# Moving one-hots and clearing to ScalarE, and 95 instead of 83 groups as dense matrices, in a four-layer graph network

## The chip, the cores and the metric

The kernel runs on one core of one Trainium2 chip. A core has five engines that run their own instruction queues and meet through semaphores: PE (TensorE, matrix products; PEld is its loading of weights), DVE (VectorE), ACT (ScalarE), POOL (GpSimd) and SP (SyncE, which here only issues DMAs). The metric is the device time of one execution in microseconds (us). Before the change it is 8078.04 us, the median of 14 runs (8072.22 to 8087.21).

## The reference, cut to what matters

There are 12500 nodes with 128 features and 200000 edges. The edges are sorted by `dst`, and `dst` is 12500 times the square of a uniform number, so low nodes have very many edges and high nodes have few. `src` is uniform. Four layers follow each other; after each, a normalization over the features of a node.

```python
# layer 0
W = silu(dist_feat @ fw1 + fb1) @ fw2 + fb2          # one row per edge, from 50 features
x = silu(h @ aw1 + ab1) @ aw2 + ab2                  # one row per node
agg = segment_sum(W * x[src], dst)
out = silu(agg @ ow1 + ob1) @ ow2 + ob2;  return h + out
# layer 1: the edges the other way round
out = segment_sum(x[dst], src)
# layer 2
agg = segment_sum(edge_weight[:, None] * x[src], dst)
h = (agg + x) @ W1.T + b1 + agg * x @ W2.T + b2;  out = leaky_relu(h, 0.2)
# layer 3: 16 relations, each with its own 128 x 128 matrix
srcs = alphas[rels] * srcs_dense[rels, src]
vrps = segment_sum(srcs, dst) + (vfts @ update)[dst] added once per edge;  out = relu(vrps)
# each layer
x = layernorm(x + layer(x))
```

Layers 1 and 2 are products of `x` with a sparse 12500 x 12500 matrix: layer 1 with the counts of edges between two nodes, layer 2 with the sums of their weights.

## The kernel before

**Edges and groups.** 512 edges make a group of four columns of 128 edges; there are NG = 391 groups and T = 1564 columns. Because the edges are sorted, the edges of a group fall into a window of 128 consecutive nodes. Each layer walks the groups from the highest to the lowest in a loop over steps `s`. In each step several stages work, each on another group: `group(k)` is the group that has reached stage `k`. Everything is written in this order into the queues of the engines (`tc.manual_schedule()`), and each engine runs its queue in order. The order of the calls in the loop body is thus the order on each engine.

**Layer 0 (steps 0 to 402).** Stage 0 loads the edge features `dt`; stage 2 computes `ph` on PE (one PSUM buffer); stage 3 applies silu on ACT (`h`, L766) and gathers 4 x 128 rows of the node table on POOL (`gather`, L305, into a buffer of the pool `xg`); stage 5 computes `pw` on PE (L770, L773); stage 7 builds one-hots of the target nodes on DVE (`one_hots`, L322) and multiplies `pw` with the gathered rows (L780); stage 8 sums them by target node on PE (L346); stage 11 adds the window to `acc` (L371). Besides, `blk.run(s)` finishes the nodes in blocks of 128, from the highest, as their last group is done: product and silu (L699), root on ACT with a reload of ACT's function tables before and after it (L639, L766), norm (L647), and stores on SP.

**Layer 1 (from step 392).** `L1 = NG + 1`. For each group, ACT builds two one-hots (L1013, L1015, L1017), PE multiplies them to counts, ACT copies the counts (L790), PE multiplies them with a window of the table, ACT copies the result into a buffer of the pool `xg` (L833), and POOL adds its rows by DMA into one of four sums in memory (`scatter_add`, L393). DVE computes the addresses (`twins_by_group`, `to`, L1026, nine buffers).

**Dense matrices for the lowest nodes.** The groups below GH = 83 hold so many edges per node that their part of the sparse matrix is built as dense blocks instead. `dense_plan()` cuts the first HC = 332 columns of edges into HBATCHES = 24 batches; each batch covers at most HS = 32 target nodes, and a batch has units of 4, 2, 1 or 0 columns (0 stands for a column that is cut into two halves of 64 edges), such that the edges of a unit lie within HW = 5 nodes. `DenseSteps` does it twice in one tile `dense` of 128 x 98 x 32 numbers: kind 0 (the counts of layer 1, in bf16 one-hots) runs in the steps of layer 0, kind 1 (the weights of layer 2, in f32) in the steps of layer 1. Per unit there are three calls:

- `make`, given in step `s`: for each column a one-hot `dense_lo` (128 wide, L930) and a one-hot `dense_hi` (490 wide, L933 for kind 1, L936 for kind 0), both on DVE, four buffers each;
- `multiply`, given in step `s + 1`: their product on PE (`du`, L951);
- `add`, taken in step `s + 2`: DVE adds `du` to five of the 32 columns of `dense` (L962).

Behind a batch whose last unit is made in step `s`, `store` (step `s + 3`) writes `dense` to memory on SP's queue (L967, 1568 KB) and `clear` (step `s + apart + 2`) sets it to zero on DVE (L971). The next batch is begun in step `s + 1 + apart`. `rate` is the number of steps from one unit (or one pair of units of four columns at most) to the next.

```python
for kind, t, apart, rate in ((0, 8.0, 4, 1.68), (1, first_weights, 3, 1.2)):
```

`todo.take(s)` runs the calls taken in a step in the middle of the loop body, behind stage 11 of layer 0; `todo.give(s, ...)` runs those given at the end, `make` last.

From step 417 on the counts are used: for each of the 98 blocks of source nodes and each of ROUNDS = 2 rounds of HB = 12 batches, SP loads a part of the counts (`dense_in`, for two blocks at a time), ACT brings it into line (`dense_line`, L986), PE transposes it (L994), ACT copies it (`dense_t`, L998), PE multiplies it with the rows of the low nodes (L1004), and DVE adds the product to `x` (L1007). One block of one round goes in each step. The weights are used in layer 2 in the same way, without a transpose (`dense_w_in`, L1212), one block of one round in each step, and their sums are added to `acc` behind that.

**Between and behind.** `nodes_1` adds up the four sums and normalizes. Layer 2 walks the groups down to GH: gathers on POOL, weighted one-hots on DVE (L328), sums on PE (L346), add to `acc` (L371); blocks of nodes are finished as their groups are done (`finish_steps`), and the table of relations for layer 3 is written. Layer 3 gathers from that table for all 391 groups. `gather` and the messages of layer 1 share the pool `xg`: seven buffers, each with the 512 rows of a group.

Of the kernel before, what the change touches and what calls it, by code (L numbers as in the profile page):

```python
# [8 lines left out]
F32 = mybir.dt.float32  # L9
# [8 lines left out]
P = 128  # L18
# [20 lines left out]
HS = 32  # L39
HB = 12  # L40
ROUNDS = 2
# [6 lines left out]
class Consts:  # L48
    def __init__(self, nc, pool):
        self.ident = pool.tile([P, P], F32, name="ident")  # L50
        make_identity(nc, self.ident)
        self.row = pool.tile([P, P], F32, name="row")
        nc.gpsimd.iota(self.row, pattern=[[1, P]], base=0, channel_multiplier=0,
                       allow_small_or_imprecise_dtypes=True)
        self.nodes = pool.tile([P, NB + 1], F32, name="nodes")
        nc.gpsimd.iota(self.nodes, pattern=[[P, NB + 1]], base=0, channel_multiplier=1,
                       allow_small_or_imprecise_dtypes=True)
        self.ones = pool.tile([P, P], F32, name="ones")
# [4 lines left out]
        nc.vector.memset(self.eps, EPS)  # L63

        self.before = pool.tile([P, P], BF16, name="before")
        nc.vector.tensor_scalar(self.before, self.row, self.nodes[:, 0:1], None, op0=OP.is_lt)
# [89 lines left out]
class Edges:  # L156
# [24 lines left out]
    def steps(self, wk, ps):  # L181
# [25 lines left out]
        base = wk.tile([1, NG], F32, name="base_f")  # L207
        nc.vector.tensor_copy(base, self.base)
        pb = by_group("pb")
        nc.tensor.matmul(pb, c.ones[0:1, :], base, start=True, stop=True)  # L210
# [4 lines left out]
        nc.tensor.matmul(px, c.ones[0:1, :], step, start=True, stop=True)  # L215
        yield
# [227 lines left out]
def kernel(ctx: ExitStack, tc: tile.TileContext, i, out):  # L444
# [204 lines left out]
    def row_block(table, b):  # L649
        return table[b * P:(b + 1) * P, :]  # L650

    def windows():
        with tc.manual_schedule():
            with tc.tile_pool(name="pa", bufs=3) as wk, tc.tile_pool(name="pas", bufs=4) as small, \
                    tc.tile_pool(name="pd", bufs=2) as dn, tc.tile_pool(name="pps", bufs=2, space=PSUM) as ps:
                layers_0_and_1(wk, small, dn, ps)
            with tc.tile_pool(name="pn", bufs=4) as wk, tc.tile_pool(name="pns", bufs=4) as small, \
                    tc.tile_pool(name="pnps", bufs=3, space=PSUM) as ps:
                nodes_1(wk, small, ps)
            with tc.tile_pool(name="pb", bufs=2) as wk, tc.tile_pool(name="pbk", bufs=1) as kp, \  # L660
                    tc.tile_pool(name="pbs", bufs=4) as small, tc.tile_pool(name="pbps", bufs=2, space=PSUM) as ps:
                layers_2_and_3(wk, kp, small, ps)
# [5 lines left out]
    def layers_0_and_1(wk, small, dn, ps):  # L668
# [20 lines left out]
        def b_copy(b):  # L689
            t = bst[b]["a"] = small.tile([P, P], F32, name="a", tag="a", bufs=2)  # L690
            nc.vector.tensor_copy(t, acc[:, b * P:(b + 1) * P])
# [5 lines left out]
        def b_silu(b):  # L697
            h = bst[b]["h"] = small.tile([P, P], F32, name="hb", tag="hb", bufs=2)
            nc.scalar.activation(h, fixed[:, 0, :], AF.Silu, bias=w.ob1)  # L699
# [34 lines left out]
        srcs = {}  # L734
        SC = 64

# [124 lines left out]
    class DenseSteps:  # L861
# [4 lines left out]
        def __init__(self, dn, ps, dense, fixed, first_weights, first_products):  # L866
# [10 lines left out]

            for kind, t, apart, rate in ((0, 8.0, 4, 1.68), (1, first_weights, 3, 1.2)):
                for b, units in enumerate(DENSE):
                    k = 0  # L880
                    while k < len(units):
# [8 lines left out]
                        t += rate  # L890
                    self.later(self.given, s + 3, self.store, kind, b)
                    self.later(self.taken, s + apart + 2, self.clear)
                    t = s + 1 + apart
# [29 lines left out]
        def make(self, kind, unit):  # L923
# [4 lines left out]
            for col in range(c0, c0 + n):  # L928
                lo = self.tile("dense_lo", P, dtype)
                nc.vector.tensor_scalar(lo, c.row, ed.dense_lo[:, col:col + 1], None, op0=OP.is_equal)  # L930
                hi = self.tile("dense_hi", J * P, dtype)[:, :NB * HW]
                if kind:
                    nc.vector.tensor_scalar(hi, self.key, ed.dense_key[:, col:col + 1], ed.dense_w[:, col:col + 1],  # L933
                                            op0=OP.is_equal, op1=OP.mult)
                else:
                    nc.vector.tensor_scalar(hi, self.key, ed.dense_key[:, col:col + 1], None, op0=OP.is_equal)  # L936
                made.append((lo, hi))
# [31 lines left out]

        def clear(self):  # L970
            nc.vector.memset(self.dense, 0.0)  # L971

# [11 lines left out]
        def line_up(self, h):  # L984
            self.line[h] = self.dn.tile([P, HB, HS], F32, name="dense_line", tag="dense_line")
            nc.scalar.copy(self.line[h], self.chunk[h // 2][:, :, h % 2, :])  # L986
# [673 lines left out]
    with tc.If(fits > 0) as arm:  # L1660
        with tc.tile_pool(name="xg", bufs=7) as gp:
            windows()
    with arm.Else():
# [52 lines left out]
```

## Time and profile before

| | |
|---|---|
| median of 14 runs | 8078.04 us |
| the profiled execution, its own time | 8083.42 us |
| span of its profile | 8081.6 us |
| PE, DVE, ACT, POOL busy | 72%, 50%, 33%, 76% of the span |
| layer 0, first to last gather | 75 to 2097 us |
| layer 1, first to last scatter | 2112 to 4426 us |
| layer 2, first to last gather | 4528 to 6076 us |
| layer 3, first gather to the end | 6109 to 8082 us |

A group of instructions is shown as: line, engine, operation, out<-in xcount | busy us, mean ns of one | idle time of the engine just ahead of them and what ended it. "issue" is time in which the engine waited for nothing that the profile shows. In a view by time, a row gives the start in us, the length in us, and in brackets the idle time ahead of it and what released it. Matmul ends are modelled, so a busy PE is not a PE at its peak. The granted clock is a share of TensorE's full speed.

### The profile page before, as it was taken

The page shows a single profiled execution, that of the slowest core. Times are in us where ns is not written, and L with a number is a line of the kernel's source. Part 1 is how long each engine was busy: PE and PEld are TensorE (multiplying, and loading weights), DVE is VectorE, ACT ScalarE, POOL GpSimd, SP SyncE. Part 2 cuts the span into 40 slices and gives each one's busy share as a digit, 9 for nine tenths or more (in the row PEclk, how much of TensorE's full clock was granted, in tenths as well). Part 3 has the DMA queues.
Part 4 walks back from the last instruction along what each step waited for, and adds up shares of the span by engine and source line. Part 5 has one row for each costly group of instructions (what it writes and reads, how often), then busy time and mean ns, then how long its engine had stood idle before and what let it go on. Part 6 is the DMA issues. An engine that isn't in the chain of part 4 may idle for free. (4 is left out here: it accounts for less than half of the span.)

```text
span 8081.6 us, 89625 instructions
## 1 busy us (share of the span) xinstructions
PE 5820.9 (72%) x24309; PEld 3794.1 (47%) x24309; DVE 4068.4 (50%) x14132; ACT 2628.1 (33%) x5986; POOL 6122.5 (76%) x5603
## 2 busy tenths in 40 slices
PE   8888888898787766777643677777776666666665
PEld 5555555555444444554332344444443444444343
DVE  6776666654576555545431444445444443433333
ACT  2333333221577776777663311111110000000000
POOL 4777777777788888888887477777776777777777
PEclk8888888777898877777555898987775555555555
DMA  5543333333467677776655666664442222222221
GB/s 152 171 153 100 99 99 92 98 94 91 86 123 134 122 130 126 123 131 111 104 89 78 213 172 168 170 170 138 131 127 71 59 58 58 57 56 55 55 54 51
DMA packets 877253, 882.01 MB, mean 109 GB/s; under 512 B 428177, under 2 KB 683624, under 8 KB 870598
## 3 DMA queue, kind: packets, MB, share of 16 engines
q0 software_dynamic: 316960, 366.85, 24.6%
q1 hardware_dynamic: 545705, 496.90, 20.3%
q10 hardware_dynamic: 14078, 12.43, 0.5%
q8 instruction: 202, 3.31, 0.2%
q14 instruction: 308, 2.52, 0.1%
HBM read 555.71 MB, written 319.97 MB: 108 GB/s over the span
## 5 line engine op out<-in xcount | busy, mean ns | idle before, releaser
L305 POOL DMA_INDIRECT xg<-table,at x2796 | 2720.7, 973 | 952.9 <-issue 730.0
L346 PE MATMUL pa<-oh,xg 128*128 128x128 f32 x5592 | 1691.0, 418 | 1052.6 <-DMA xg<-rel_table,at 623.5
L393 POOL DMA_INDIRECT sums<-xg,to x1232 | 1913.6, 1553 | 414.8 <-issue 295.8
L346 PEld LDWEIGHTS pa<-oh,xg 128*128 128x128 f32 x5592 | 1185.8, 273 | 1638.3 <-issue 717.3
L305 POOL DMA_INDIRECT xg<-rel_table,at x1564 | 1485.3, 950 | 477.1 <-issue 374.5
L371 DVE TENSOR_TENSOR acc<-acc,pa 128x128 f32 x1090 | 305.9, 281 | 1422.4 <-PE pa L346 1365.9
L328 DVE TENSOR_SCALAR oh<-row,drel,wgt 128x128 f32<-128x128 f32 x2796 | 793.2, 359 | 34.3 <-PE pa L346 26.5
L951 PE MATMUL du<-dense_hi,dense_lo 128*128 128x490 f32 (+3 forms) x1239 | 706.2, 661 | 86.9 <-DVE dense L962 85.0
L647 ACT ACTIVATE x<-x,off,rs 128x128 f32<-128x128 f32 x294 | 144.9, 493 | 1392.1 <-DVE off L646 1384.5
L830 PE MATMUL fixed<-oh,one_b 128*1 128x128 bf16 x1216 | 144.9, 256 | 595.7 <-DVE m L1021 591.3
L783 PE MATMUL ph<-dt,fw 50*128 50x512 f32 x782 | 500.2, 723 | 75.2 <-ACT h L766 67.5
L773 PE MATMUL pw<-fw,h 128*128 128x128 f32 x3128 | 552.6, 330 | 0.0
L773 PEld LDWEIGHTS pw<-fw,h 128*128 128x128 f32 x3128 | 466.1, 229 | 115.0 <-issue 115.0
L346 PE MATMUL pa<-oh,m 128*128 128x128 f32 x3128 | 505.1, 315 | 12.8 <-DVE acc L371 12.8
L346 PEld LDWEIGHTS pa<-oh,m 128*128 128x128 f32 x3128 | 474.0, 232 | 14.6 <-DVE acc L371 14.1
L639 ACT ACTIVATE rs<-mv,eps 128x1 f32<-128x1 f32 x294 | 86.8, 295 | 1203.9 <-DVE mv L634 1185.9
L962 DVE TENSOR_TENSOR dense<-dense,du 128x490 f32 x646 | 427.8, 662 | 91.4 <-PE du L954 71.2
L1026 DVE TENSOR_TENSOR to<-n_ahead,at 128x4 int32<-128x4 f32 x308 | 50.6, 164 | 838.8 <-DMA sums<-xg,to 833.4
L780 DVE TENSOR_TENSOR m<-pw,xg 128x512 f32<-128x512 f32 x391 | 268.0, 685 | 395.0 <-DMA xg<-table,at 375.4
L1013 ACT ACTIVATE oh<-row,drel 128x128 bf16<-128x128 f32 x1216 | 388.7, 394 | 218.4 <-PE fixed L830 213.1
L1161 PE MATMUL pr<-wrel,x 128*128 128x512 f32 x784 | 435.5, 685 | 2.3 <-ACT x L1153 2.3
L766 ACT ACTIVATE h<-ph,fb 128x512 f32<-128x512 f32 x391 | 266.6, 682 | 510.2 <-PE ph L783 508.1
(205 smaller groups left out, 8436.2 us busy)
## 6 DMA issues: line engine op xcount, KB each, us to landing
rel_table<-tb SPq DMA_DIRECT2D x196, 512.0 KB
dt<-in_src_r SPq DMA_DIRECT2D x308, 256.0 KB
xg<-table,at POOLq DMA_INDIRECT x2796
dt<-in_dfT SPq DMA_DIRECT2D x391, 100.0 KB
dense_counts<-dense SPq DMA_DIRECT2D x24, 1568.0 KB
dense_in<-dense_counts SPq DMA_DIRECT2D x98, 384.0 KB
dense_weights<-dense SPq DMA_DIRECT2D x24, 1568.0 KB
dense_w_in<-dense_weights SPq DMA_DIRECT2D x96, 384.0 KB
```

The source lines that it names most:

```text
L305: nc.gpsimd.indirect_dma_start(out=x[:, j, :], out_offset=None, in_=table, in_offset=bass.IndirectOffsetOnAxis(ap=idx[:, j:j + 1], axis=0))
L328: nc.vector.tensor_scalar(oh[:, j, :], c.row, at[:, j:j + 1], weight[:, j:j + 1], op0=OP.is_equal, op1=OP.mult)
L346: self.nc.tensor.matmul(pa, x[:, j, :], oh[:, j, :], start=j == 0, stop=j == J - 1)
L371: nc.vector.tensor_add(to, to, pa)
L393: nc.gpsimd.indirect_dma_start(out=accs[(first + j) % len(accs)], out_offset=bass.IndirectOffsetOnAxis(ap=to[:, j:j + 1], axis=0), in_=msg ...
L773: nc.tensor.matmul(pw[:, j, :], h[:, j * P:(j + 1) * P], w.fw2, start=False, stop=j == J - 1)
L780: nc.vector.tensor_mul(ms[g], pws.pop(g), xgs.pop(g))
L783: nc.tensor.matmul(phs[g], w.fw1, dts.pop(g), start=True, stop=True)
L951: nc.tensor.matmul(pk[:, :NB * HW], lo[part], hi[part], start=j == 0, stop=j == len(made) - 1)
L962: nc.vector.tensor_tensor(to, to, pk[:, :NB * HW].rearrange("p (h n) -> p h n", n=HW), op=OP.add)
L1013: nc.scalar.activation(pair[:, 0, j, :], c.row, AF.Abs, bias=at[:, j:j + 1], scale=-1.0)
L1161: nc.tensor.matmul(pr, t["x3"], wrel[:, k:k + 4, :], start=True, stop=True)
```

## The change

It has five parts.

1. HB goes from 12 to 16. With that there are 32 batches, HC = 380 columns and GH = 95 groups. The 48 new columns are all of kind "0": two halves each, so 96 more products and adds for each kind. Layers 1 and 2 walk 296 groups, not 308. The tiles that hold all batches of a round are a third wider: `dense_in`, `dense_line`, `dense_t`, the product of layer 2 (512 columns, not 384).
2. The times of `DenseSteps`: `rate` 1.68 becomes 1.32 and 1.2 becomes 1.0; `apart` 4 becomes 3 and 3 becomes 2; `store` is given in step `s + 2`, not `s + 3`.
3. `make` of kind 0 builds each one-hot on ACT with two instructions, Abs of the difference and Relu of one less that, instead of one comparison on DVE.
4. `clear` is two copies of a zero on ACT, each of half of `dense`, in steps `s + 4` and `s + apart + 2`, instead of one memset on DVE.
5. Room in SBUF: the pool `xg` has six buffers in layers 0 and 1 (seven in layers 2 and 3, where it is opened anew behind `nodes_1`); `a`, `hb` and `dense_line` have one buffer, not two; the sources are loaded and converted for 16 columns at a time, not 64 (`sources`, DMA on SP, cast on ACT); `ones` is one column, and a row of ones is made where it is needed.

```diff
-HB = 12
+HB = 16
...
-            with tc.tile_pool(name="pa", bufs=3) as wk, tc.tile_pool(name="pas", bufs=4) as small, \
+            with tc.tile_pool(name="xg", bufs=6) as gp, tc.tile_pool(name="pa", bufs=3) as wk, tc.tile_pool(name="pas", bufs=4) as small, \
...
-            with tc.tile_pool(name="pb", bufs=2) as wk, tc.tile_pool(name="pbk", bufs=1) as kp, \
+            with tc.tile_pool(name="xg", bufs=7) as gp, tc.tile_pool(name="pb", bufs=2) as wk, tc.tile_pool(name="pbk", bufs=1) as kp, \
...
-            t = bst[b]["a"] = small.tile([P, P], F32, name="a", tag="a", bufs=2)
+            t = bst[b]["a"] = small.tile([P, P], F32, name="a", tag="a", bufs=1)
...
-            h = bst[b]["h"] = small.tile([P, P], F32, name="hb", tag="hb", bufs=2)
+            h = bst[b]["h"] = small.tile([P, P], F32, name="hb", tag="hb", bufs=1)
...
-        SC = 64
+        SC = 16
...
-            for kind, t, apart, rate in ((0, 8.0, 4, 1.68), (1, first_weights, 3, 1.2)):
+            for kind, t, apart, rate in ((0, 8.0, 3, 1.32), (1, first_weights, 2, 1.0)):
...
-                    self.later(self.given, s + 3, self.store, kind, b)
-                    self.later(self.taken, s + apart + 2, self.clear)
+                    self.later(self.given, s + 2, self.store, kind, b)
+                    self.later(self.taken, s + 4, self.clear, 0)
+                    self.later(self.taken, s + apart + 2, self.clear, 1)
...
-                nc.vector.tensor_scalar(lo, c.row, ed.dense_lo[:, col:col + 1], None, op0=OP.is_equal)
                 hi = self.tile("dense_hi", J * P, dtype)[:, :NB * HW]
                 if kind:
+                    nc.vector.tensor_scalar(lo, c.row, ed.dense_lo[:, col:col + 1], None, op0=OP.is_equal)
                     nc.vector.tensor_scalar(hi, self.key, ed.dense_key[:, col:col + 1], ed.dense_w[:, col:col + 1],
                                             op0=OP.is_equal, op1=OP.mult)
                 else:
-                    nc.vector.tensor_scalar(hi, self.key, ed.dense_key[:, col:col + 1], None, op0=OP.is_equal)
+
+                    for to, of, at in ((lo, c.row, ed.dense_lo), (hi, self.key, ed.dense_key)):
+                        nc.scalar.activation(to, of, AF.Abs, bias=at[:, col:col + 1], scale=-1.0)
+                        nc.scalar.activation(to, to, AF.Relu, bias=c.ones[:, 0:1], scale=-1.0)
...
-        def clear(self):
-            nc.vector.memset(self.dense, 0.0)
+        def clear(self, k):
+
+            half = self.dense.rearrange("p h n -> p (h n)")[:, k * NB * HS // 2:(k + 1) * NB * HS // 2]
+            nc.scalar.copy(half, c.zero.to_broadcast([P, NB * HS // 2]))
...
-            self.line[h] = self.dn.tile([P, HB, HS], F32, name="dense_line", tag="dense_line")
+            self.line[h] = self.dn.tile([P, HB, HS], F32, name="dense_line", tag="dense_line", bufs=1)
...
-        with tc.tile_pool(name="xg", bufs=7) as gp:
-            windows()
+        windows()
```

More of the change, by code (lines that the diff above doesn't have):

```diff
@@ L57, in __init__ @@
                        allow_small_or_imprecise_dtypes=True)
-        self.ones = pool.tile([P, P], F32, name="ones")
+        self.ones = pool.tile([P, 1], F32, name="ones")
         nc.vector.memset(self.ones, 1.0)
@@ L63, in __init__ @@
         nc.vector.memset(self.eps, EPS)
+        self.zero = pool.tile([P, 1], F32, name="zero_c")
+        nc.vector.memset(self.zero, 0.0)
         self.before = pool.tile([P, P], BF16, name="before")
@@ L208, in steps @@
         nc.vector.tensor_copy(base, self.base)
+        ones = wk.tile([1, P], F32, name="ones_row")
+        nc.vector.memset(ones, 1.0)
         pb = by_group("pb")
-        nc.tensor.matmul(pb, c.ones[0:1, :], base, start=True, stop=True)
+        nc.tensor.matmul(pb, ones, base, start=True, stop=True)
         step = wk.tile([1, NG], F32, name="step")
@@ L214, in steps @@
         px = by_group("px")
-        nc.tensor.matmul(px, c.ones[0:1, :], step, start=True, stop=True)
+        nc.tensor.matmul(px, ones, step, start=True, stop=True)
         yield
@@ L650, in row_block @@
         return table[b * P:(b + 1) * P, :]
+    gp = None
     def windows():
+        nonlocal gp
         with tc.manual_schedule():
-            with tc.tile_pool(name="pa", bufs=3) as wk, tc.tile_pool(name="pas", bufs=4) as small, \
+            with tc.tile_pool(name="xg", bufs=6) as gp, tc.tile_pool(name="pa", bufs=3) as wk, tc.tile_pool(name="pas", bufs=4) as small, \
                     tc.tile_pool(name="pd", bufs=2) as dn, tc.tile_pool(name="pps", bufs=2, space=PSUM) as ps:
```

## The prediction, made before the result was known

> **What bounds the kernel now.** I read the busy time by stage first, then the costliest groups, then single engines in order of time where two of them meet. Stages, in order: two parts of layer 0, the dense part of layer 1, layer 2 (columns: stretch, length, busy PE, PEld, DVE, ACT, POOL with instruction counts, granted clock, DMA share, GB/s).
>
> ```profile
> 98.00:400.00 302.00, 268.03 (x1311) 169.28 (x1310) 217.32 (x744) 93.15 (x134) 229.59 (x238) 0.88 0.49 153
> 800.00:2097.00 1297.00, 1125.92 (x5169) 751.16 (x5168) 757.45 (x2430) 379.90 (x564) 991.92 (x1002) 0.81 0.33 95
> 2246.00:3770.00 1524.00, 1111.55 (x5973) 735.42 (x5972) 844.56 (x2482) 1125.11 (x2869) 1254.89 (x808) 0.81 0.70 126
> 4528.00:6077.00 1549.00, 1126.07 (x4377) 736.12 (x4377) 742.72 (x2822) 220.45 (x572) 1173.62 (x1232) 0.84 0.54 152
> ```
>
> POOL looks 76 to 82% busy, but the rest is the issue of its own next DMA. In order of time its gathers of layer 0 start every 1.25 us with "issue" between them, and one thing only disturbs them (POOL, then DVE):
>
> ```profile
> 551.59 0.95 POOL L305 DMA_INDIRECT xg<-table,at  x1 [0.30 <-DVE oh L322]
> 552.84 3.99 POOL L305 DMA_INDIRECT xg<-table,at  x1 [0.30 <-issue]
> 557.13 0.94 POOL L305 DMA_INDIRECT xg<-table,at  x1 [0.30 <-issue]
> ...
> 553.26 2.67 DVE L971 MEMSET dense<- 128x3136 f32 x1 [0.60 <-issue]
> ```
>
> A gather that meets the clearing of `dense` takes 4 us, not 0.94. So POOL sets the pace: 4 x 1.25 = 5.0 us a step in layers 0 and 2 (measured in layer 2: 1.257 us from start to start), and 4 x 1.85 = 7.4 us in layer 1, whose scatters start every 1.85 us. Layer 3 is the same gathers and is not touched. Cheaper work on another engine gains nothing unless it shortens POOL; dearer work costs nothing until it falls behind POOL's pace. PE runs its steps in 3.4 to 4.3 us where nothing stops it (starts of `h` at 121.30, 124.65, 128.93, 132.28). ACT is the engine with room in layer 0, and has little in layer 1.
>
> **The change part by part**, against the profiled execution's own 8083.4 us, which is 5.4 us above the median 8078.0.
>
> *Clears leave DVE (layer 0).* 24 starts of gathers in layer 0 lie over 1.6 us apart, each at an L971; what they exceed 1.25 by sums to 56 us. On ACT the copies run beside POOL as its silus do: -56. Ends: 0 (a copy holds POOL as well) and -56. The scatters of layer 1 keep 1.54 us and a pitch of 1.85 beside a clear, so nothing there.
>
> *Counts' one-hots leave DVE.* Gathers away from the clears exceed 0.94 us by 19 us in total; the 233 beside L936 by 0.04 each. -9, ends 0 and -19.
>
> *The same one-hots on ACT.* A column is Abs and Relu of 128, Abs and Relu of 490, each Relu waiting for its Abs. The rows:
>
> ```profile
> L1013 ACT ACTIVATE oh<-row,drel 128x128 bf16<-128x128 f32 x1136 | 363.1, 395 | 165.3 <-PE fixed L830 160.1 <-DVE n_ahead L1024 5.2
> L766 ACT ACTIVATE h<-ph,fb 128x512 f32<-128x512 f32 x383 | 261.1, 682 | 475.6 <-PE ph L783 473.5
> L639 ACT ACT_TABLE_LOAD x97 | 124.5, 1283 | 1.7
> ...
> 2610.00 1.26 ACT L1015 ACTIVATE oh<-dt,src_f 128x128 bf16<-128x128 int32 x4
> 2611.29 1.15 ACT L1017 ACTIVATE oh<-oh,ones 128x1024 bf16<-128x1024 bf16 x1
> ...
> 150.90 1.12 PE L783 MATMUL ph<-dt,fw 50*128 50x512 f32 x2
> 151.95 1.00 PE L951 MATMUL du<-dense_hi,dense_lo 128*128 128x490 bf16 x4
> ```
>
> Independent activations follow each other 0.1 us before the end (4 of 128 in 1.27); a dependent one 0.03 after it (1017 after 1015). So 0.39 + 0.03, then 0.30, then 0.67 (490 wide, between 0.395 and 0.682) + 0.03, then 0.58: 2.0 us a column, 8.0 for a step of four. Four columns fill all four buffers of `dense_lo` and `dense_hi`, so the next make waits for the first product of the last one, which PE issues after `ph`, and `ph` has one buffer and waits for the silu behind the last make. The loop of such a step: silu 0.69, then `ph` and the first product, 1.5 us at the clock of this row and 2.2 at 0.6 of full speed (I take 1.9, since PE will wait more and the clock is 0.57 where PE is half busy, at 3770 to 4427 us), then 8.0. That is 10.6 us, against POOL's 5.0.
>
> In steps 8 to 63 (the first four batches) there are 34 make-steps of four columns: 360 us. Two of two columns at 4.7: 9. Four gaps of three steps without a make, at PE's pace (silu, three `ph` of 1.12, products 0.93, twice 2.2 of `pw` and `pa`): 9.4 each, 37. Six halves of a clear at about 1.55 (1568 elements, by the slope from 128 to 1024 wide): 9. The first half waits for the store, which is issued one step later than it could be by little: a store issued at 2294.1 released its clear at 2302.7, so 8.6 us, some 5 of them waited, three times: 15. Fourteen blocks with two table loads, root, norm and silu, 3.5 each, one hidden in every gap: 35. Together 465 us for 56 steps that POOL does in 280: 185 late. POOL is level with ACT at step 8 (its group 4.75 at 98.5 us) and six buffers let it run two steps ahead of DVE, which is 1.5 ahead of ACT: 3.5 steps, 17 us, are free. 168 remain. Behind that, a batch of ten steps with two-column makes is 6 x 4.7 + 1.9 + 9.4 + clears 3.1 + store 5 + two blocks 7 = 54 against 50; the nine batches to step 158 differ, and I put 3 on each: 27. From step 159 on a make is one column and ACT has room. +195. Ends: ACT's instructions back to back without any wait, at 1.73 a column, are 326 us for 56 steps: +29; with the clock at 0.5 and 8 us on each later batch: +290. I take the value by the loop because each of its waits has a named queue.
>
> A rule beside that row: the Trainium skill, "TensorE: Matmul & The Clock Gate", Part 1, has the clock at full or at half, by whether PE was busy in the last window, with no value between. The trace's stages lie between (0.81, 0.57) as means. By the rule a PE that waits most of each loop would be at half: 0.8 us more in 34 loops and 28 in the gaps, which would make the sum 55 us larger.
>
> *96 more half-column products, 96 more adds, earlier rates (layer 0).* PE 96 x 0.43 and DVE 96 x 0.66 less 319 us of L930, L936, L971: behind POOL, nothing. Without that cover, PE at 89% would bind first.
>
> *12 fewer groups in layer 1.* 48 scatters at 1.85: -89, with their DMAs on SP, copies, one-hots and twins. *32 stores of weights, not 24:* 15 long gaps of POOL just after a store sum to 24 us; eight more stores, +8 (ends 0 and +30, as the loads of counts grow by a third while DMA is 70% busy). *ACT in layer 1:* a step of the products runs 2608.40 to 2614.65 when ACT is pressed, 6.25 us. To it come 0.2 (two copies 512 wide, not 384), 0.2 (a fourth transpose ahead of it), 0.34 (two half clears in nine steps), 0.28 (55 more casts of sources, 0.23 + 1.28 waited each, over 296 steps; SP issues each one step ahead at most) and about 0.27 (a clear behind its store, 2.5 us in nine steps): 7.54 against 7.4. In the 209 steps of the products: +29, ends 0 and +60. What is queued behind these ACT waits is the copy of counts and of messages, so PE's products and POOL's scatters; four steps of lead in `to` cover single waits, not a rate.
>
> *12 fewer groups in layer 2.* 48 gathers at 1.257: -60. The dense product widens from 384 to 512, 0.15 us on PE twice a step: behind POOL. Tail between the layers: the last block starts 10 steps behind the last gather, not 8: two light steps, +3, ends 0 and +6. POOL's idle 33 us there stays otherwise, as do the 101 us at the norm.
>
> *Fewer buffers, reopened pools, smaller constants:* `xg` 6 is counted above; one buffer for `a`, `hb` and `dense_line` puts back-to-back uses three steps, or one, apart: 0 (up to +5 in layer 1).
>
> Sum: 8083.4 - 56 - 9 + 195 - 89 + 8 + 29 - 60 + 3 = 8104; less 5.4 for the median: **8099 us**.
>
> **The rivals.** *Faster: the loop is shorter than its parts.* If makes cost little more than ACT's own instructions (+60 and not +195) and layer 1 stays with POOL, the sum is 7935. For it: POOL has run at 1.25 us through every other disturbance, and ACT is 30% busy there. Against: one buffer of `ph` and four of the one-hots. It decides from +173 in steps 8 to 158 downward (layer 1 as forecast). *Slower by more: layer 1 passes to ACT.* +60 there, DMA gaps +30, the loop as forecast: 8150; with the clock at half in layer 0, 8205. For it: ACT's 74% in the third window. Against: POOL's waits for ACT are nearly nil now. *The change doesn't do what it says: the ACT copy holds POOL as the memset did.* +56 and a third more for 32 batches: 8174. Against it: no gather is long beside an ACT instruction.
>
> **How the numbers follow.** Forecast 0.42, own range 8050 to 8150; faster 0.35, centred on 7950; layer 1 on ACT 0.18; POOL held 0.05. This kernel's runs tell about 0.2%, 16 us. From these: faster 0.36 (the rival and the low edge of the forecast), within 16 us 0.15, slower 0.49. Two in ten left out at the edges of both outer cases gives 7965 to 8200.
>
> **What would show it.** Right: gathers in the first 600 us that wait, with ACT over 85% busy there and starts of `h` some 10 us apart in make-steps; no gather over 2 us beside a clear; 296 x 7.4 us of scatters; layer 2 about 58 us shorter. Wrong: POOL at 1.25 us from step 8 on; or scatters apart by more than 1.95 us on average between 2300 and 3800; or a granted clock that stays at 0.88 in the first batches, which would take 40 us off the loop.

## The result, and the profile after

| | |
|---|---|
| median after | 8166.72 us (8152.51 to 8174.23, 6 runs) |
| median before, same chip | 8077.56 us |
| ratio | 1.0108, 95% interval 1.0098 to 1.0118 |
| span of the profile after | 8173.9 us (before 8081.6) |

The change makes the kernel slower by 1.1%: 89 us, where 21 were forecast. The stages, read from the starts of POOL's instructions (us):

| stretch | before | after | difference | forecast |
|---|---|---|---|---|
| layer 0, first to last gather | 2022.4 | 2229.5 | +207 | +130 |
| layer 1, first to last scatter | 2313.5 | 2247.1 | -66 | -52 |
| layer 2, first to last gather | 1547.9 | 1484.7 | -63 | -60 |
| last gather of layer 2 to first of layer 3 | 33 | 50 | +17 | +3 |
| all else | | | -3 | 0 |

The forecast of layer 0 is -56 -9 +195, that of layer 1 -89 +8 +29. Layer 0 differs most from what was said, by 77 us. Layer 1 and the tail behind layer 2 differ by 14 each, with opposite signs.

The stages after, as they were shown of before (stretch, length, busy PE, PEld, DVE, ACT, POOL with instruction counts, granted clock, DMA share, GB/s); the first rows are layer 0:

```profile
98.00:250.00 152.00, 104.55 (x387) 61.51 (x387) 36.25 (x119) 120.79 (x236) 76.59 (x82) 0.72 0.22 65
250.00:500.00 250.00, 170.22 (x633) 101.55 (x632) 74.51 (x261) 192.42 (x352) 101.92 (x109) 0.69 0.32 102
500.00:750.00 250.00, 197.42 (x836) 126.32 (x836) 109.07 (x380) 183.44 (x317) 142.64 (x152) 0.77 0.47 151
750.00:1000.00 250.00, 204.61 (x966) 129.93 (x965) 131.26 (x445) 203.48 (x349) 171.36 (x181) 0.86 0.34 101
...
2320.00:4566.00 2246.00, 1713.71 (x8624) 1098.21 (x8623) 1189.17 (x3636) 1684.76 (x4050) 1835.70 (x1183) 0.77 0.69 124
4668.00:6153.00 1485.00, 1106.37 (x4234) 697.51 (x4235) 717.18 (x2734) 211.98 (x556) 1124.49 (x1184) 0.85 0.60 162
```

Read the last count in the second row: 109 gathers in 250 us, 2.3 us each, where POOL's own pace gives 200. ACT is 77 to 80% busy in the first two rows, PE 68 to 69%, and the granted clock is 0.69 to 0.72, where the first 300 us of layer 0 had 0.88 before. From 750 us on the counts approach POOL's pace. One make of four columns in order of time (start, length, engine, line; in brackets the idle time ahead):

```profile
128.61 0.67 ACT L773 ACTIVATE h<-ph,fb 128x512 f32<-128x512 f32 x1
129.33 2.07 PE L790 MATMUL ph<-dt,fw 50*128 50x512 f32 x2 [4.64 <-ACT h L773]
131.33 1.81 PE L962 MATMUL du<-dense_hi,dense_lo 128*128 128x490 bf16 x4
131.96 0.40 ACT L946 ACTIVATE dense_lo<-row,dense_lo 128x128 bf16<-128x128 f32 x1 [2.68 <-PE du L962]
...
139.59 0.70 ACT L947 ACTIVATE dense_hi<-dense_hi,ones 128x490 bf16<-128x490 bf16 x1
139.81 0.94 POOL L309 DMA_INDIRECT xg<-table,at  x1 [5.43 <-DVE m L787]
140.19 0.67 ACT L773 ACTIVATE h<-ph,fb 128x512 f32<-128x512 f32 x1
140.92 2.07 PE L790 MATMUL ph<-dt,fw 50*128 50x512 f32 x2 [3.66 <-ACT h L773]
```

From silu to silu 11.58 us, in a step that POOL does in 5. Each piece of the loop in the prediction is here: silu, `ph` behind it, the first product, ACT's 2.68 us of waiting for that product, and four columns in 8.23 us. PE stands 3.66 us for the next silu, and POOL 5.43 us for a buffer of `xg` that DVE's product `m` has to free. Over layer 0 the waits of POOL and PE come to this (waits: us in total, times, longest):

```profile
POOL xg L309 <- DVE m L787: 272.9, 69, 11.9
POOL xg L309 <- DVE acc L375: 28.7, 22, 6.1
...
PE ph L790 <- ACT h L773: 248.1, 94, 8.7
```

In layer 0 of the kernel before, no wait of POOL is over 0.4 us; what disturbs it there are the long gathers beside a clear. "Lateness" below is the time by which a stretch of layer 0's gathers exceeds 1.25 us each: 276 us after, 69 before.

### The profile page after: what moved, and what is told of

It is laid out like the page before. It is cut to its first block, busy times and chain, and to the rows that moved or that the text cites. A ratio compares the mean times of both kernels' runs of the same rounds, so it can differ in the third digit from the quotient of the medians.

```text
span 8173.9 us, 92453 instructions
## 1 busy us (share of the span) xinstructions
PE 6074.7 (74%) x24993; PEld 3879.0 (47%) x24993; DVE 3878.4 (47%) x13749; ACT 3545.8 (43%) x7545; POOL 5929.6 (73%) x5507
## 4 chain that ended last, share of the span: by engine, by line
POOL 24%; PE 20%; DMA 20%; issue 16%; ACT 12%; DVE 7%; DVEq 1%; SPq 0%; ACTq 0%; POOLq 0%
POOL xg L309 18%; DMA sums<-xg,to 7%; POOL sums L397 6%; DMA xg<-rel_table,at 5%; DMA xg<-table,at 5%; PE pa L350 5%; PE du L962 3%; PE pw L780 3%; PE ph L790 3%; DVE dense L973 2%; ACT dense_hi L947 2%; PE pr L1174 2%; ACT dense_hi L946 2%; DMA dense_counts<-dense 1%; ACT dense_lo L947 1%
## 5 line engine op out<-in xcount | busy, mean ns | idle before, releaser
L309 POOL DMA_INDIRECT xg<-table,at x2748 | 2604.9, 948 | 1211.7 <-issue 726.6
L350 PE MATMUL pa<-oh,xg 128*128 128x128 f32 x5496 | 1652.9, 418 | 993.6 <-DMA xg<-rel_table,at 606.8
L397 POOL DMA_INDIRECT sums<-xg,to x1184 | 1838.1, 1552 | 424.7 <-issue 274.0
L350 PEld LDWEIGHTS pa<-oh,xg 128*128 128x128 f32 x5496 | 1164.5, 274 | 1563.1 <-issue 713.0
L962 PE MATMUL du<-dense_hi,dense_lo 128*128 128x490 f32 (+3 forms) x1527 | 886.7, 673 | 38.3 <-DVE dense L973 38.0
L790 PE MATMUL ph<-dt,fw 50*128 50x512 f32 x782 | 532.8, 766 | 255.7 <-ACT h L773 248.1
L973 DVE TENSOR_TENSOR dense<-dense,du 128x490 f32 x838 | 555.0, 662 | 78.4 <-PE du L965 44.4
L1174 PE MATMUL pr<-wrel,x 128*128 128x512 f32 x784 | 419.1, 662 | 6.0 <-ACT x L1166 6.0
L1179 ACT COPY tb<-pr 128x512 f32<-128x512 f32 x196 | 114.7, 585 | 639.5 <-PE pr L1174 623.4
```

Of the source, the lines that this page charges most:

```text
L309: nc.gpsimd.indirect_dma_start(out=x[:, j, :], out_offset=None, in_=table, in_offset=bass.IndirectOffsetOnAxis(ap=idx[:, j:j + 1], axis=0))
L350: self.nc.tensor.matmul(pa, x[:, j, :], oh[:, j, :], start=j == 0, stop=j == J - 1)
L397: nc.gpsimd.indirect_dma_start(out=accs[(first + j) % len(accs)], out_offset=bass.IndirectOffsetOnAxis(ap=to[:, j:j + 1], axis=0), in_=msg ...
L790: nc.tensor.matmul(phs[g], w.fw1, dts.pop(g), start=True, stop=True)
L962: nc.tensor.matmul(pk[:, :NB * HW], lo[part], hi[part], start=j == 0, stop=j == len(made) - 1)
L973: nc.vector.tensor_tensor(to, to, pk[:, :NB * HW].rearrange("p (h n) -> p h n", n=HW), op=OP.add)
```

## The experiments

The ratio is always to the kernel before on the same chip; lateness and stages are those of the profiled execution.

| run | median us | ratio (95%) | lateness in steps 8-63 | 64-158 | layer 0 in all | gap to layer 3 |
|---|---|---|---|---|---|---|
| before | 8078 | 1 | 5 | 20 | 69 | 33 |
| after | 8167 | 1.0108 (1.0098-1.0118) | 201 | 64 | 276 | 50 |
| e1_hots_on_dve | 7935 | 0.9815 (0.9799-0.9831) | 2 | 18 | 27 | 53 |
| e2_clear_only | 8029 | 0.9932 (0.9915-0.9948) | 2 | 5 | 14 | 33 |
| e3_hots_only | 8182 | 1.0120 (1.0104-1.0137) | 103 | 44 | 169 | 34 |
| e4_groups_only | 8010 | 0.9905 (0.9888-0.9921) | 11 | 33 | 100 | 50 |
| e5_big_on_dve | 7960 | 0.9853 (0.9833-0.9873) | 3 | 53 | 60 | 53 |
| e6_spread | 8130 | 1.0064 (1.0042-1.0085) | 89 | 108 | 230 | 49 |
| e7_fill_late | 8174 | 1.0118 (1.0098-1.0138) | 198 | 41 | 265 | 54 |
| e8_two_per_buffer | 8112 | 1.0038 (1.0025-1.0050) | 146 | 62 | 209 | 53 |

**The parts by themselves.** First the changed kernel with the counts' one-hots back on DVE and the clears left on ACT:

```diff
-                    for to, of, at in ((lo, c.row, ed.dense_lo), (hi, self.key, ed.dense_key)):
-                        nc.scalar.activation(to, of, AF.Abs, bias=at[:, col:col + 1], scale=-1.0)
-                        nc.scalar.activation(to, to, AF.Relu, bias=c.ones[:, 0:1], scale=-1.0)
+                    nc.vector.tensor_scalar(lo, c.row, ed.dense_lo[:, col:col + 1], None, op0=OP.is_equal)
+                    nc.vector.tensor_scalar(hi, self.key, ed.dense_key[:, col:col + 1], None, op0=OP.is_equal)
```

> The changed kernel, with the counts' one-hots built on DVE again by one comparison each (clears stay on ACT, 95 groups, new rates, six buffers). Theory A (the make loop on ACT in layer 0 is the loss: POOL waited 275 us more than its own pace there): those waits fall to under 30, layer 0 from first to last gather takes about 1965 us and the whole about 7900. Theory B (the closer schedule and the six buffers of gathered rows are the loss, on whatever engine the one-hots are): layer 0 stays over 2150 us and the whole over 8080.

7935 us, 1.9% faster than before. Layer 0 is 249 us shorter than after, the other stages as after (layer 1 2246.2, layer 2 1483.2). The loss of the change thus lies wholly in this one part, and all the others together gain 1.9%. The same stretch of it as above:

```profile
250.00:500.00 250.00, 214.21 (x1007) 137.30 (x1005) 174.83 (x597) 94.68 (x128) 181.11 (x191) 0.86 0.55 176
```

191 gathers for 109, with ACT at 38% and the clock at 0.86.

The kernel before with the clear as two half copies on ACT, nothing else:

```diff
-            nc.vector.memset(self.dense, 0.0)
+            for k in range(2):
+                nc.scalar.copy(flat[:, k * NB * HS // 2:(k + 1) * NB * HS // 2], c.zero.to_broadcast([P, NB * HS // 2]))
```

> The kernel before with one part of the change: dense is cleared by two half copies on ACT at the step of the memset. If the memset held POOL and the copy does not: no gather over 1.3 us, 56 us less, 8022. If a copy on ACT holds POOL as well: 8078 and long gathers remain. If ACT's 3 us at a clear delay the silu and with it POOL: more than 8078.

Layer 0 falls from 2022.4 to 1967.8 us, no gather lasts over 1.3 us, layers 1 and 2 keep their times. That is -55 us, where the term said -56. The groups of gathers of this kernel, and its copies (groups: busy us, mean ns of one, idle):

```profile
L307 POOL DMA_INDIRECT xg<-table,at x1547 | 1476.0, 954 | 471.5 <-issue 404.5 <-DVE oh L324 14.3 <-DMA xg<-table,at 14.3
L975 ACT COPY dense<-zero_c 128x1568 f32<-128x1568 f32 x48 | 69.2, 1493 | 0.0
```

The kernel before with only the counts' one-hots on ACT (the lines removed in the first diff, in its place), at the old rate of units and 83 groups:

> The kernel before with one part of the change: the counts' one-hots by Abs and Relu on ACT, at the old rate of 1.68 steps. Theory A: a make-step of four columns takes 11 to 12 us on ACT, the first four batches run about 130 us late: 8200. Theory B (only the closer schedule hurts): 8070 to 8090.

+1.2%. The lateness of layer 0 rises by 100 us, although the gathers beside a clear cost 23 us now and not 56. So the one-hots cost by themselves, and more so at the new rate.

The changed kernel with both the one-hots and one clear on DVE, that is the 95 groups, their times and their buffers only:

```diff
-                    self.later(self.taken, s + 4, self.clear, 0)
-                    self.later(self.taken, s + apart + 2, self.clear, 1)
+                    self.later(self.taken, s + apart + 2, self.clear)
...
+            nc.vector.memset(self.dense, 0.0)
```

> The changed kernel with one-hots and clearing both on DVE as before, so only 95 groups, rates and buffers are new. Theory A: layers 1 and 2 shorten by 68 and 58 us, 32 memsets hold POOL in layer 0 where 24 did (19 us more): 7970. Theory B: layer 0 is late by 100 us and more: 8050 to 8150.

-0.95%. 32 memsets now hold POOL, and the mean gather of layer 0 shows it against the line above (1005 ns for 954):

```profile
L309 POOL DMA_INDIRECT xg<-table,at x1515 | 1522.7, 1005 | 471.0 <-issue 395.6 <-DVE m L787 14.7 <-DMA xg<-table,at 13.1
L980 DVE MEMSET dense<- 128x3136 f32 x32 | 85.5, 2672 | 19.3 <-issue 15.6 <-DVE acc L375 2.4 <-DMA xg<-table,at 1.2
```

The long gathers exceed 0.94 us by 78 us in sum, and between e4 and e1, which differ by the clears alone, there are 74 us. The clears are worth what they take of POOL, per batch.

**Which makes.** DVE for the units of four and two columns, ACT for single and halved ones:

```diff
+                elif n > 1:
+                    nc.vector.tensor_scalar(lo, c.row, ed.dense_lo[:, col:col + 1], None, op0=OP.is_equal)
+                    nc.vector.tensor_scalar(hi, self.key, ed.dense_key[:, col:col + 1], None, op0=OP.is_equal)
```

> The changed kernel, with the counts' one-hots on DVE for units of four and two columns and on ACT for the single and halved columns. Theory A (the four-column loop in steps 8 to 63 is the loss): POOL's 201 us of waits there go, the 64 us of steps 64 to 158 fall under 20, 7925 to 7945, as with all one-hots on DVE. If the single columns on ACT hurt by themselves, by ACT's steady load: 7990 and more.

7960 us: the large makes account for 216 of the 249 us; the single and halved ones on ACT still cost 33 against e1, nearly all of it in steps 64 to 158.

**What in a make costs.** From step 21 on SP issues DMAs of zeros (`fill`) that read from `acc`, and DVE's additions to `acc` wait for them. In the changed kernel, from 98 to 590 us (waits as above):

```profile
DVE acc L375 <- DMA sums<-acc: 42.2, 16, 6.4
```

Here these DMAs begin in step 171:

```diff
-                if s > 20 and fill:
+                if s > 170 and fill:
```

> The changed kernel with the zeroing of the four sums in memory begun in step 171, not 21. In steps 21 to 92 DVE's add to acc waits for the DMA that reads zeros out of acc (43 us in the first 500). If these waits lie on the loop now: 8130 to 8155. If ACT's loop hides them: 8167.

The waits are gone, and the lateness in steps 8 to 63 is 198 us for 201: they are not what sets the time.

Next, two columns of one-hots in each of the four buffers, so that a make doesn't wait for the product of the one before it:

```diff
-                lo = self.tile("dense_lo", P, dtype)
-                hi = self.tile("dense_hi", J * P, dtype)[:, :NB * HW]
...
+                    if (col - c0) % 2 == 0:
+                        los = self.dn.tile([P, 2, P], dtype, name="dense_lo", tag="dense_lo", bufs=4)
+                        his = self.dn.tile([P, 2, J * P], dtype, name="dense_hi", tag="dense_hi", bufs=4)
+                    lo, hi = los[:, (col - c0) % 2, :], his[:, (col - c0) % 2, :NB * HW]
```

> The changed kernel with two columns of the counts' one-hots in each buffer (a half of its room is empty with bf16), so that eight columns fit and a make does not wait for the first product of the last one. If that wait (2.7 us seen, 1.9 forecast) is part of the loop: some 90 us less in steps 8 to 63, 8080. If ACT's instructions alone set the pace: 8167.

The wait is gone: a make follows its silu at once. The expected -90 took 34 waits of 2.7 us. ACT's waits of the changed kernel from 98 to 590 us have fewer, since a make that follows a light step finds its buffers free:

```profile
ACT dense_lo L946 <- PE du L962: 53.1, 24, 2.7
ACT x L651 <- DVE off L650: 26.3, 4, 8.8
```

53.1 us, and the lateness in these steps falls by 55, from 201 to 146: the wait is worth what it lasts. The whole is 8112 us, for the 8080 expected. What stays, in order of time, with two columns in a buffer:

```profile
309.44 0.68 ACT L773 ACTIVATE h<-ph,fb 128x512 f32<-128x512 f32 x1
310.17 2.07 PE L790 MATMUL ph<-dt,fw 50*128 50x512 f32 x2 [4.14 <-ACT h L773]
...
322.66 0.69 ACT L773 ACTIVATE h<-ph,fb 128x512 f32<-128x512 f32 x1
323.38 0.94 POOL L309 DMA_INDIRECT xg<-table,at  x1 [7.94 <-DVE m L787]
323.40 2.07 PE L790 MATMUL ph<-dt,fw 50*128 50x512 f32 x2 [5.81 <-ACT h L773]
```

13.2 us from silu to silu, in which ACT never waits: half a clear (1.49), four columns (8.2) and a block's root with two table loads (2.85). PE stands 5.81 us for that silu and comes back at half its pace (`ph` 2.07 us; 1.12 at the full clock).

Third, the makes of three or four columns get three steps each, so that ACT's sum of work in three steps is far below POOL's 15 us:

```diff
-                        t += rate
+                        t += rate if kind else 3.0 if sum(max(m, 1) for _, m in units[k - n:k]) > 2 else 1.0
```

> The changed kernel with the same instructions, but in counts three steps from a make of three or four columns to the next and one step from smaller ones, so that ACT's load is spread (last make in step 389, not 366). Theory A (the peak of the load decides, not its sum): nearly all of the 276 us of POOL's waits go, 7920 to 7960. If the sum of ACT's work decides: 8140 to 8170.

8130 us: the expectation, 7920 to 7960, was missed by a wide margin, and with it the idea that ACT's density is all that counts. Three steps with one make, in order of time:

```profile
304.78 0.69 ACT L773 ACTIVATE h<-ph,fb 128x512 f32<-128x512 f32 x1
305.52 2.07 PE L790 MATMUL ph<-dt,fw 50*128 50x512 f32 x2 [6.62 <-ACT h L773]
307.63 0.69 ACT L773 ACTIVATE h<-ph,fb 128x512 f32<-128x512 f32 x1 [1.78 <-PE ph L790]
...
313.92 0.68 ACT L773 ACTIVATE h<-ph,fb 128x512 f32<-128x512 f32 x1
314.49 0.40 ACT L946 ACTIVATE dense_lo<-row,dense_lo 128x128 bf16<-128x128 f32 x1
...
325.74 0.69 ACT L773 ACTIVATE h<-ph,fb 128x512 f32<-128x512 f32 x1
326.48 2.07 PE L790 MATMUL ph<-dt,fw 50*128 50x512 f32 x2 [6.62 <-ACT h L773]
```

21.0 us from `ph` to `ph` three steps on, where POOL needs 15, with ACT idle for over 7 of them (1.78 in these lines, 5.33 ahead of a block's silu at 313.65). The step with the make takes ACT's queue, 11.8 us here, while PE stands 6.6. The two light steps take PE's own pieces, 2.9 and 6.3 us: `ph` and the product at half the clock behind that stop, and a round of `pw` and `pa`, with a block's silu behind DVE. `ph` has one buffer, and the silu that frees it stands behind the whole make in ACT's queue, so the two don't overlap. From silu to silu, on average over steps 8 to 63 (the two steps of two columns left out):

| | steps with four columns | steps without a make |
|---|---|---|
| after, 98 to 590 us | 34 of 11.5 us | 20 of 4.3 us |
| e8_two_per_buffer, 100 to 537 us | 34 of 9.9 us | 20 of 4.3 us |
| e6_spread, 98 to 482 us | 19 of 11.1 us | 37 of 4.7 us |

So a step takes about the longer of ACT's queue and PE's pieces, and a long one is not made up by light ones, which are only 0.3 to 0.7 us shorter than POOL's 5.0. By that e6 should be 19 x 6.1 - 37 x 0.3 = 105 us late there, less what the buffers of `xg` give, against the 89 seen.

How much of this is ACT's sum of work can be read from the same 56 steps, for which POOL needs 280 us (columns as above; after, e8_two_per_buffer, e6_spread):

```profile
98.00:590.00 492.00, 338.79 (x1276) 202.23 (x1276) 142.83 (x492) 373.86 (x693) 219.44 (x234) 0.71 0.31 97
...
100.00:537.00 437.00, 326.36 (x1279) 197.62 (x1279) 143.68 (x495) 371.85 (x694) 220.33 (x234) 0.74 0.35 110
...
98.00:482.00 384.00, 278.13 (x1209) 171.88 (x1209) 123.97 (x463) 239.77 (x433) 220.84 (x235) 0.78 0.37 113
```

After and in e8 ACT's own work is 374 and 372 us, so some 90 us of the lateness would be there however well the makes overlapped with PE; the rest is time in which ACT waits. In e6 ACT works for 240 us, less than POOL needs, and the steps still take 384: there the sum explains nothing, and the excess of single steps over POOL's pace explains the lateness. No run gives `ph` a second buffer or puts the silu elsewhere in ACT's queue, so that this hand-over is to blame is read from the waits and from e6, and not shown by removing it.

**Makes of at most two columns, and the tail.** With the packed buffers, units of four columns made two and two in neighbouring steps, units of two not paired, so that the sum of ACT's work is that of the change:

```diff
+                        split = not kind and units[k][1] == 4
...
+                            if split:
+                                self.later(self.given, s, self.make, kind, u, 0, 2)
+                                s += 1
+                                self.later(self.given, s, self.make, kind, u, 2, 4)
...
+                        t += rate if kind else 2.6 if split else 1.3 if units[k][1] else 1.0
```

> The changed kernel with two columns of one-hots in each buffer, and with no step that makes more than two columns on ACT: a unit of four columns is made two and two in neighbouring steps, units of two are not paired, and the units follow each other at 2.6 steps for four columns and 1.3 for two. The sum of ACT's work is that of the changed kernel (8167 us), spread over all of layer 0. Theory (a make adds to PE's chain of pieces only by what it exceeds the roughly 3 us that PE works beside it; two columns, 4.1 us, exceed it by about 1): the lateness of layer 0's gathers in steps 8 to 63 is 30 to 70 us, well below the 146 us with the same buffers and four columns a step, and the whole comes to 7950 to 8010. Rival (ACT's sum of work sets the pace, however it is cut): lateness in layer 0 of 180 us or more and 8090 us or more in all.

And the first experiment's kernel (one-hots on DVE) with the finishing blocks of layer 2 two steps apart, not three:

```diff
-        blk = Blocks(finish_steps(7, 0, 3, GH, HBLOCKS, ROUNDS * (NB + HB) + 2))
+        blk = Blocks(finish_steps(7, 0, 2, GH, HBLOCKS, ROUNDS * (NB + HB) + 2))
```

> The kernel with 95 groups and the counts' one-hots on DVE (7935 us), with the units of the finishing blocks of layer 2 two steps apart instead of three. Early blocks then end sooner (from step 249 on), and three blocks (steps 296, 302, 304) instead of four stand behind the last gather at 295. Theory (the tail is blocks that are crowded behind the last gather): the gap from layer 2's last gather to layer 3's first falls from 53 to 35 to 45 us and the whole to 7915 to 7930. Rival (the gap is the last block's own chain, or the blocks' work is then only denser in front of the gathers): the gap stays at 50 to 55 and the time at 7935, or layer 2's gathers lengthen by as much as the gap gives.

Both were run once more, since these two runs met a condition that no run above shows: the kernel before took 9251 us in them, and 9243 in the repetition. In layer 0 of these four runs 121 to 134 starts of gathers lie over 3.5 us apart, most often twelve gathers from one to the next.

> The kernel of e10_split once more, on a chip whose layer 0 isn't paced by those stalls if one is to be had. Theory (a make lengthens PE's chain by what it exceeds the roughly 3 us of PE's other pieces): lateness in layer 0 in steps 8 to 63 of 30 to 70 us (146 with four columns in a step, e8_two_per_buffer), whole time 7950 to 8010, ratio 0.984 to 0.992. Rival (ACT's sum of work sets the pace however it is cut): lateness in layer 0 of 180 us or more, 8090 us or more, ratio 1.0015 or more.

> The kernel of e9_tail once more, since e9_tail and e10_split ran on a chip on which the kernel before took 9251 us and layer 0 of both was paced by stalls of 4 to 9 us that come with every 16th gather or so and are in no other run. There the gap behind layer 2's last gather was 41 us with the blocks two steps apart and 60 us with them three apart (e10_split). Theory (blocks crowded behind the last gather): gap 35 to 42 against 53 us with the blocks three apart, ratio to the kernel before 0.979 to 0.981 (7910 to 7925 of 8078). Rival (the gain is given back in layer 2): gap as before or layer 2 longer by 10 us or more, ratio 0.9815.

| run | median us | ratio (95%) | layer 0 | layer 2 | gap to layer 3 |
|---|---|---|---|---|---|
| e9_tail | 9105 | 0.9856 (0.9835-0.9878) | 2631.1 | 1724.6 | 41.2 |
| e10_split | 9117 | 0.9862 (0.9841-0.9882) | 2653.4 | 1718.5 | 59.6 |
| e11_tail_again | 9111 | 0.9852 (0.9833-0.9872) | 2633.4 | 1724.7 | 42.4 |
| e12_split_again | 9118 | 0.9871 (0.9855-0.9888) | 2628.2 | 1719.0 | 61.2 |

The absolute numbers of the expectations can't be held against these; the two kernels can be held against each other. The tail: blocks two steps apart shorten the gap by 18 and 19 us, and layer 2 is 6 us longer for it in both pairs. The two kernels of a pair differ in layer 0 too, but that lies far ahead of the tail. So the tail is blocks crowded behind the last gather, and 12 to 13 us of it can be had; the theory holds, with a third of its gain given back.

The split: the kernel with all of the counts' one-hots on ACT has layer 0 at 2653 and 2628 us, the one without any at 2631 and 2633. In steps 8 to 63 the lateness is 99 and 97 us with them, 95 and 101 without. The windows and PE's waits, from 98 to 700 us, of the kernel with one-hots on DVE (e11_tail_again):

```profile
98.00:700.00 602.00, 467.84 (x1913) 295.24 (x1913) 332.62 (x1140) 160.54 (x219) 335.87 (x353) 0.74 0.40 125
...
PE ph L790 <- ACT h L773: 31.8, 12, 9.5
```

and of the split one (e12_split_again):

```profile
98.00:700.00 602.00, 469.15 (x1881) 299.33 (x1881) 202.40 (x754) 400.79 (x717) 337.95 (x358) 0.74 0.38 117
...
PE ph L790 <- ACT h L773: 33.6, 15, 9.8
```

ACT is 67% busy for 27%, and PE waits for silu hardly longer: 33.6 us for 31.8, with as many gathers done. ACT at 67% thus costs nothing at this pace, where the changed kernel with ACT at 77% did its gathers at 2.3 us. It doesn't settle the rest: at 1.68 us a gather there are 6.7 us for a step, and the split moves makes out of steps 8 to 63 as well, where ACT now works for 257 us and not 374. In the trace of after, two steps of two columns with no more than a block's norm or silu beside them, at 607.84 and 612.92 us, take 5.1 and 4.9 us from silu to silu, just POOL's pace; a table load or half a clear on top would be late at 5.0 and hides in 6.7. What the split makes cost at POOL's own pace is open; no run here shows it.

The fastest kernel shown is e1_hots_on_dve, 1.85% faster than before. By the pairs above blocks two steps apart would give it another 12 us, an estimate, as that wasn't measured at the usual pace.

## Why the prediction was right, and where its sizes were off

Slower was forecast, by the loop of silu, `ph`, first product and make, and that loop is in the trace. The time alone wouldn't tell: 8167 us lies above the forecast's own range of 8050 to 8150 and next to the 8174 of the rival in which the copies hold POOL. What tells is that no gather of layer 0 takes over 1.12 us after, where 24 took 2.1 to 4.1 us before. Of the signs named for the loop, the make-steps are there (11.5 us), but ACT is 76% busy in steps 8 to 63 and not over 85%, since it waits more. By its steps:

- *Clears leave DVE*, -56: right. -55 alone (e2), -74 with 32 batches (e4 to e1). An ACT copy of 1.49 us doesn't lengthen a gather; the rival in which it does falls.
- *Counts' one-hots leave DVE*, -9: not measured apart from their cost on ACT. No run separates it.
- *The one-hots on ACT*, +195: right in kind, and the term that was undersized. Between e1 and after it is +249 us. In lateness: 201 us in steps 8 to 63 (forecast 168), 64 in steps 64 to 158 (27, and e1 has 18 there without any of it), 10 behind (0). The working of the first part can be laid beside the silus of the trace, from 97.77 to 590.35 us, 56 steps: 492.6 us, where 465 were forecast. Its parts (us):

| part of steps 8 to 63 | forecast | measured |
|---|---|---|
| 34 steps of four columns, without the rows below | 360 | 361 |
| two steps of two columns | 9 | 16 |
| twelve steps in the gaps between batches, without table loads | 37 + 15 | 52 |
| eight steps without a make inside the batches, without table loads | none | 19 |
| six halves of a clear | 9 | 9 |
| table loads (in the forecast with root, norm and silu) | 35 | 36 |

The sum counted 34 + 2 + 12 = 48 steps for 56. The eight that it left out, where `rate` skips a step (the first from 140.19 us), are most of the missing 28 us. That the gaps agree is luck: of the 15 us of waiting for stores there is 1.1, and instead `normed` of a block waits on ACT for DVE (the 26.3 us above), where DVE waits for the zeros of `fill`. e7 takes these waits of DVE away, and the steps without a make get 14 us shorter in sum; the gathers of these steps gain only 3. The buffers of `xg` gave 11 us and not 17. In steps 64 to 158 two-column makes were put at 4.7 us; they measured 4.9 and more, so that a table load or clear beside one is late almost in full, and these 95 steps take 538 us from silu to silu for the 475 of POOL.

- *The clock.* The Trainium skill, "TensorE: Matmul & The Clock Gate", Part 1, has the clock at full or half and nothing between, and the prediction put that at 55 us more than its own value between the two. The rows agree with the page: of the 391 pairs of `ph` 275 take 1.1 or 1.2 us and 84 take 2.1, the product takes 1.8 or 1.0, a window's 0.69 is a mean over both, and ACT's wait is 2.7 us behind a slow pair and 1.5 behind a fast one. The 1.9 of the forecast, 65 us over 34 loops, still was too much and not too little, since ten of the makes wait for nothing: 53 us. That the larger sum by the page comes near the measured +249 is by that account chance.
- *12 fewer groups in layer 1*, -89 +8 +29: measured -66. Scatters stand 1.900 us apart for 1.879, which is 24 us on 1183, and 48 of them at 1.88 are 90. The terms said +37 for these 24; no run splits them into DMA gaps and ACT. POOL's waits for ACT's messages rose as said, to 21.3 us in 22 times behind the first scatter, while the largest entry for ACT of before is 9.6. Layer 1 stayed with POOL; the rival of ACT as its bound falls.
- *12 fewer groups in layer 2*, -60: measured -63. *The dense product's width* shows in no stage.
- *The tail*, +3: measured +17. The step counted how far behind the last gather the last block starts. What counts is how many blocks are crowded there: with 95 groups four blocks (steps 296, 299, 302, 305) follow the last gather, in step 295; e9_tail and e11_tail_again shorten the gap by having three.
- *Fewer buffers*, 0: not measured by itself. In e1 eleven waits of POOL for DVE ahead of a gather, all between 370 and 550 us, exceed the usual 0.3 us by 16 us in sum; in e2, with seven buffers of `xg` and the old rate, there is none.

The rival of a shorter loop (7935) did not come. That e1 measures 7935 as well is chance, since it has no loop at all. The forecast's other terms without the one-hots' move give 165 us less than before, and e1 is 149 us below the kernel before on its chip: layer 0 gained 42 us for 56 and the tail lost 20 for 3, while layers 1 and 2 gained 20 more than said.

## What to carry to other kernels

Before moving work to an idle engine, look for a one-deep hand-over between that engine and the pacing chain in the same in-order queue: here silu frees `ph`. Cost the move step by step, as the excess of each step over the pace of the bounding engine, and not by the idle share of the engine (ACT was 30% busy in layer 0): a chain that is 89% busy on PE makes up little in its light steps, so spreading whole pieces over time helps little (276 us late became 230), while cutting them below the pace may, which no run here shows. A stalled PE is paid for again, as it restarts at half the clock (`ph` 2.07 us for 1.12).

## What the runs showed of the hardware that was not expected

- A memset of 128x3136 f32 on DVE (2.67 us) holds POOL's indirect gather (0.94 becomes 2.1 to 4.1 us), and the same clearing as two copies on ACT (1.49 us each) doesn't. Why was not tried.
- In the last four runs all kernels were slower by about 14%: layer 0 of e9_tail by a third (2631 us for the 1981 of e1_hots_on_dve), layer 2 by 16% and layer 3 by 14%, while layer 1 took the same 2242 to 2248 us. Where this was read, instructions keep their lengths and stand further apart. A pair in layer 3 on DVE, where `wgt` follows `att`, from 7000 to 7500 us, first in e1_hots_on_dve:

```profile
L1296 DVE TENSOR_TENSOR wgt<-wgt,att 128x64 f32<-128x64 f32 x90 | 20.2, 225 | 3.1
```

then in e9_tail:

```profile
L1296 DVE TENSOR_TENSOR wgt<-wgt,att 128x64 f32<-128x64 f32 x83 | 18.8, 227 | 57.5 <-remote 33.5 <-DVE att L1293 18.9 <-issue 3.7
```

225 and 227 ns of work, but 57.5 us of idle time ahead for 3.1, most of it put down to a releaser that the trace can't name. One of the two chips had run e5 to e8 at the usual pace, so the chip by itself doesn't make it. What it is stays open.
